# Earlier slots for the first block of a state-space recurrence inside a macaron MoE kernel

## The chip, the cores and the metric

The kernel runs on one core of a Trainium2 chip. The metric is the device time of one execution, in microseconds; several runs are given by their median. A profile is one further execution, with a record of every instruction; its span is the time from the first to the last record.

## What is computed

Input x is 4 sequences of 1024 tokens with 128 features. Three residual layers follow each other:

```python
x = x + 0.5 * ffn(layernorm(x))     # 8 experts, dense, weighted by router * gate
x = x + mamba(layernorm(x))         # selective state-space layer
x = x + 0.5 * ffn(layernorm(x))     # the same experts again
```

The FFN computes for each of 8 experts `silu(h @ w_gate) * (h @ w_up) @ w_down` (128 to 512 to 128 features) and sums the experts with per-token weights. The mamba layer projects to 256 channels, convolves along the sequence with 4 taps, applies silu, derives from the result a step width `dt` (softplus) and two 16-vectors B and C per token, and runs for each channel and each of 16 states n

```python
h = exp(dt * A[n]) * h + dt * xc * B[n];   y += h * C[n]
```

along the sequence; y is then gated and projected back.

## The kernel before, in words

The 4096 tokens are cut into 8 blocks of 512 (two per sequence, so even blocks start a sequence). An FFN pass over one block is 16 **steps**; a step handles two chunks of 128 hidden features of one expert. There are 16 passes (each block once for the first FFN, once for the second), so 256 steps, numbered from 0 here. Passes 0 to 3 are the first FFN of blocks 0 to 3; pass 4 is the second FFN of block 0, and so on.

In a step TensorE (PE) makes a gate group `pg` of six matmuls (L641 to L643, products of split fp32 numbers: high by high, low by high, high by low), an up group `pu` of six, and two `down` products `pd` of the step before (L722, plain fp32, two passes each). ScalarE (ACT) takes silu of `pg` into `h` (L625); VectorE (DVE) multiplies `h` by `pu` (L657). `pg` and `pu` have one PSUM buffer each: the gate group of the next step waits for this step's silu, the up group of the next step waits for this step's multiplication. When an expert is done ACT copies `pd` to SBUF (`take`, L735), which frees the single `pd` buffer; GpSimd (POOL) weights and sums it (L744, L747). In steps 2 to 19 and near the end the down products use split numbers as well (L697, L705), with extra work on ACT and DVE.

The mamba layer of a block is threaded between the FFN steps. Its parts in `mamba_events`: transposing (`tr`), the x projection in two halves (`xsproj`, evacuated by ACT at L909), the convolution (`conv`: first tap on ACT at L921, three taps on DVE at L931, per half), two z halves (`zproj`, L1047), `act` (silu of the convolution, L948), `xproj` (the product `dbl` at L954, evacuated by ACT at L957 and L959, its low part made by DVE at L963, and B and C sent through DRAM by SyncE, L968 and L821, to be broadcast over the partitions), `dtproj` (products `v`, ACT at L979), `softplus` (L986), `dtfin` (`dx = dt * xc`, for block 0 on DVE at L991; two ACT items for `y`, L994). Then come the states: `two` makes the exponentials of two states with four ACT instructions (L1002), here called a **bundle**. Per state DVE has a product (L1015), two scans (L1021), a copy of the last column (L1032, even blocks) and a read-out (L1033); POOL adds the result into y (L1036). All the small matmul results share one PSUM buffer, `misc`. A change of ACT function between silu, softplus and exp needs an ACT_TABLE_LOAD.

The instruction order of each engine is fixed when the program is built, by a planner. A step has four **slots** (slot = 4 x step + 0 to 3). Before each slot `run_events` runs those events of each chain that are due. An event has a slot, and may have a condition; if the condition does not hold the event waits, but at most `WAIT` = 12 slots (99 for the bundles), after which it runs regardless. `START[k]` is the base slot of block k (72 for block 0, 144 for block 1), and the tuple `FRONT[0]` (or `REST`, for other blocks) gives the offsets of ten events: `ta` transposing, `xs` x projection, `cv` convolution, `ap` act, `xp` xproj, `dp` dtproj, `sp` softplus, `df` dtfin, `n0` the first bundle. The later bundles are due at n0 + 8 * int(1.56 q). `fast` is true for block 0 only.

ACT work that is not urgent is put on a list (`plan.act_put`) and emitted when the planner sees a gap, or when somebody needs it (`act_need`); `act_run` emits it at once. DVE work goes on lists `hi` and `lo` (the states' work) and is emitted in between by planned times. Conditions that matter here: `quiet` (L1098) lets softplus run only in slots that are 5 modulo 8; `turn` (L1124) lets a bundle run only in such slots, if no softplus is wanted and no other burst has run in this slot, and if at most `QUEUE` = 9 items are on the DVE list `lo`. `exps` stores the tile of state n in `d["da", n]` (L1000), and `read` pops it again (L1028).

Of the kernel before, what the change touches and what calls it, by code (L numbers as in the profile page):

```python
# [20 lines left out]
TOL = 0.4  # L21
START = (72, 144, 232, 328, 432, 544, 656, 744)
REST = (4, 9, 17, 19, 23, 25, 29, 35, 37)
FRONT = {0: (5, 7, 8, 15, 16, 18, 21, 27, 29)}
ZT = {0: 11}
SOON = (0, 4, 6, 14, 15)
CALM = (4, 5)
# [145 lines left out]
def tile_macaron_mamba_moe(  # L173
# [32 lines left out]
    ND = DI // 128  # L206
# [11 lines left out]
    plan = Plan()  # L218

    def big(name):  # L220
        return sb.tile([P, 2, TB], F32, tag="big", bufs=BIG, name=name)
# [604 lines left out]
    riders, slot, burst_at, want = [], [0], [-1], set()  # L826
# [33 lines left out]
    def mamba_events(k):  # L860
        d = {}
# [53 lines left out]
        def conv(i):  # L915
            if i == 0:
                d["cv"] = big(f"cv_{nm}")
            cv, xs = d["cv"], d["xs"]
            assert d["xsp"] > i
            def first_tap():  # L920
                S.activation(  # L921
                    cv[:, i, :], xs[:, i, 0:TB], AF.Identity,
                    bias=cb_sb[:, i : i + 1], scale=cw_sb[:, i, 0:1],
                )
                plan.put(lambda: tap(1), 0.71, plan.act + 0.61)

            it = plan.act_put(first_tap, 0.61, 0.0)
            d.setdefault("cv_it", []).append(it)

            def tap(q):  # L930
                V.scalar_tensor_tensor(  # L931
                    cv[:, i, :], xs[:, i, q : q + TB], cw_sb[:, i, q : q + 1], cv[:, i, :],
                    ALU.mult, ALU.add,
                )
                if q < 3:
                    plan.put(lambda: tap(q + 1), 0.71)
                else:
                    d["conv"] = d.get("conv", 0) + 1
                    d["cv_at"] = plan.dve + 0.1
# [149 lines left out]
        fast = k == 0  # L1089
# [5 lines left out]
        zt = ZT.get(k, 14)  # L1095
        ta, xs, cv, ap, xp, dp, sp, df, n0 = FRONT.get(k, REST)

        def quiet():  # L1098
            if d.get("dtp") != ND or slot[0] % 8 != 5:
                return False  # L1100
            want.add(k)
            return burst_at[0] < slot[0]
# [5 lines left out]
            (xs, inproj),  # L1108
            (xs, lambda: xsproj(0), lambda: max(free(), d["xlow"][4] if d["xlow"][3] else NEVER)),
            (cv, lambda: conv(0)),  # L1110
            (xs + 2, lambda: xsproj(1), free),
            (cv + 2, lambda: conv(1)),
            (zt, lambda: zproj(0), free),
            (zt + 2, lambda: zproj(1), free),
            (ap + w, act, lambda: d["cv_at"] if d.get("conv") == ND else NEVER),
            (xp + w, xproj, lambda: max(free(), d["xc_at"])),
            (dp + w, lambda: dtproj(0), lambda: max(free(), d["low"][4] if d["low"][3] else NEVER)),
            (dp + w + 2, lambda: dtproj(1), free),
            (sp + w, softplus, lambda: 0.0 if quiet() else NEVER),
            (df + w, dtfin),  # L1120
        ]
        mid = []

        def turn():  # L1124
            fits = "dx_it" in d and slot[0] % 8 == 5 and burst_at[0] < slot[0]
            return 0.0 if fits and not want and len(plan.lo) <= QUEUE else NEVER

        for q in range(NS // 2):
            def two(q=q):
                burst_at[0] = slot[0]  # L1130
                while riders:
                    riders.pop(0)()
                exps(2 * q)
                exps(2 * q + 1)

            mid += [(n0 + 8 * int(SPR * q) + w, two, turn)]
# [103 lines left out]
```

## Time and profile before

| quantity | value |
|---|---|
| median of 3 runs | 1266.12 us (1266.01 to 1266.13) |
| time of the profiled execution | 1265.99 us |
| its span | 1264.2 us |
| POOL busy | 706.1 us, 56% |
| DMA | 115.09 MB, 91 GB/s on average |
| steps 16 to 31 (pass 1) | 85.1 us from 81.5 to 166.6 us |
| passes 2, 3, 4 | 81.4, 78.0 and 79.6 us |

The pass times are differences between the starts of the L657 multiplications of steps 16, 32, 48, 64 and 80 in the trace. Block 0's front part (transposing to softplus) lies in steps 21 to 26, its states in steps 27 to 51; block 1's front part begins at step 37.

How to read the profile: a line of the timeline has start (us from the span's start), length, engine, source line, operation, output and inputs, shape, and a count if consecutive instructions were merged; in square brackets the idle time of the engine before it and who ended it. Durations of matmuls overlap, so for PE the distance between starts is what counts. A row of the table by stages has the stage, its length, and then for PE, PE's weight loads (PEld), DVE, ACT and POOL the busy time with the number of instructions, the granted clock, and the DMA share with GB/s.

### The profile page before, as it was taken

What the parts mean: (1) busy time and instruction counts of PE and PEld (TensorE: products, weight loads), DVE (VectorE), ACT (ScalarE), POOL (GpSimd) and SP (SyncE); (2) the same over time, 40 slices, a digit from 0 to 9 for tenths busy, and PEclk for the clock granted to TensorE, in tenths of its full rate; (3) what the DMA queues carried; (4) which work ended last, traced back from release to release, by engine and by line L of the source; (5) the groups of instructions that cost most, each with busy time, mean ns of one, the idle gap of its engine ahead of it and who ended that gap; (6) DMA issues with size and microseconds to landing.
All of it is one profiled execution on the core that took longest, in us unless ns stands there. A gap on an engine that the chain in (4) does not pass through costs nothing.

```text
span 1264.2 us, 14417 instructions
## 1 busy us (share of the span) xinstructions
PE 1245.2 (99%) x4800; PEld 862.0 (68%) x4800; DVE 1138.2 (90%) x1286; ACT 921.8 (73%) x1326; POOL 706.1 (56%) x557
## 2 busy tenths in 40 slices
PE   9999999999999999999999999999999999999998
PEld 7776666666666666666666666666666666668787
DVE  6985699999899999999999999999999999998676
ACT  7684887776777768787788778778777776666653
POOL 1022465757568647775676567757775676554400
PEclk9999999999999999999999999999999999999999
DMA  4501333343343433334343353432433433311011
GB/s 147 158 26 34 107 112 86 101 112 82 81 107 97 118 91 95 93 99 110 99 100 96 92 119 84 120 98 82 113 98 79 110 92 109 103 56 42 26 43 25
DMA packets 75386, 115.09 MB, mean 91 GB/s; under 512 B 7472, under 2 KB 23728, under 8 KB 75312
## 3 DMA queue, kind: packets, MB, share of 16 engines
q1 hardware_dynamic: 75312, 114.19, 33.6%
q8 instruction: 37, 0.61, 0.2%
q14 instruction: 37, 0.30, 0.1%
HBM read 109.71 MB, written 4.46 MB: 90 GB/s over the span
## 4 chain that ended last, share of the span: by engine, by line
PE 70%; DVE 16%; ACT 5%; issue 5%; POOL 3%; DMA 1%; SPq 0%; DVEq 0%; ACTq 0%; POOLq 0%
PE pd L722 19%; PE pu L641 7%; PE pg L641 7%; PE pg L643 7%; PE pu L643 7%; PE pu L642 7%; PE pg L642 7%; DVE hb_m L1021 5%; DVE h L657 4%; PE pd L697 3%; DVE hb_m L1015 2%; DVE da_m L1033 2%; PE pd L705 1%; ACT da_m L1002 1%; ACT h L625 1%
## 5 line engine op out<-in xcount | busy, mean ns | idle before, releaser
L722 PE MATMUL pd<-h,wd 128*128 128x512 f32 x824 | 391.6, 592 | 1.2 <-ACT tmp L735 1.2
L657 DVE TENSOR_TENSOR h<-h,pu 128x1024 f32<-128x1024 f32 x256 | 311.1, 1215 | 76.9 <-PE pu L643 52.5
L1036 POOL TENSOR_TENSOR y_m<-y_m,da_m 128x1024 f32<-128x1024 f32 x128 | 310.5, 2426 | 106.5 <-DVE hb_m L1015 103.2
L625 ACT ACTIVATE h<-pg 128x1024 f32<-128x1024 f32 x256 | 262.7, 1026 | 140.2 <-PE pg L643 135.2
L641 PE MATMUL pg<-xh_f,wh 128*128 128x512 f32 x510 | 266.9, 523 | 0.7 <-ACT h L625 0.7
L744 POOL TENSOR_TENSOR tmp<-tmp,cwb 128x512 f32<-128x512 f32 x98 | 129.1, 1318 | 196.6 <-issue 106.2
L722 PEld LDWEIGHTS pd<-h,wd 128*128 128x128 f32 x824 | 153.5, 188 | 107.9 <-issue 89.6
L641 PE MATMUL pu<-xh_f,wh 128*128 128x512 f32 x512 | 205.8, 402 | 5.8 <-DVE h L657 5.6
L643 PE MATMUL pg<-xh_f,wl 128*128 128x512 f32 x510 | 201.1, 394 | 0.8 <-DVE wl L299 0.8
L643 PE MATMUL pu<-xh_f,wl 128*128 128x512 f32 x512 | 200.5, 392 | 0.0
L642 PE MATMUL pu<-xl_f,wh 128*128 128x512 f32 x512 | 199.9, 391 | 0.0
L642 PE MATMUL pg<-xl_f,wh 128*128 128x512 f32 x510 | 199.4, 391 | 0.0
L1015 DVE TENSOR_TENSOR hb_m<-dx_m,bcb_m 128x1024 f32<-128x1024 f32 x128 | 166.4, 1300 | 1.8
L1021 DVE TENSOR_TENSOR_SCAN hb_m<-da_m,st_sb,hb_m 128x512 f32<-128x512 f32 x128 | 164.2, 1283 | 2.3
L1002 ACT ACTIVATE da_m<-dt_m,A_sb 128x512 f32<-128x512 f32 x256 | 164.0, 711 | 0.6
L1021 DVE TENSOR_TENSOR_SCAN hb_m<-da_m,hb_m 128x512 f32<-128x512 f32 x128 | 156.7, 1224 | 2.6
L1033 DVE TENSOR_TENSOR da_m<-hb_m,bcb_m 128x1024 f32<-128x1024 f32 x128 | 155.8, 1217 | 1.5
L641 PEld LDWEIGHTS pg<-xh_f,wh 128*128 128x128 f32 x510 | 96.0, 188 | 64.8 <-issue 27.4
L747 POOL TENSOR_TENSOR acc<-acc,tmp 128x512 f32<-128x512 f32 x98 | 130.3, 1330 | 7.6
L642 PEld LDWEIGHTS pg<-xl_f,wh 128*128 128x128 f32 x510 | 96.3, 189 | 50.6 <-issue 36.5
L641 PEld LDWEIGHTS pu<-xh_f,wh 128*128 128x128 f32 x512 | 96.1, 188 | 35.4 <-DVE h L657 15.8
L643 PEld LDWEIGHTS pg<-xh_f,wl 128*128 128x128 f32 x510 | 95.6, 187 | 23.2 <-DVE wl L299 1.2
(181 smaller groups left out, 1494.7 us busy)
## 6 DMA issues: line engine op xcount, KB each, us to landing
bcb_m<-bc_m SPq DMA_DIRECT2D x128, 512.0 KB
cwb<-cd_f SPq DMA_DIRECT2D x128, 256.0 KB
out_dram<-x SPq DMA_DIRECT2D x13, 256.0 KB
x<-in_L_attn_x_dram SPq DMA_DIRECT2D x8, 256.0 KB
wraw<-in_L_ffn_w_gate_dram SPq DMA_DIRECT2D x8, 256.0 KB
wraw<-in_L_ffn_w_up_dram SPq DMA_DIRECT2D x8, 256.0 KB
wd<-in_L_ffn_w_down_dram SPq DMA_DIRECT2D x8, 256.0 KB
cd_f<-ct_f SPq DMA_DIRECT2D x64, 4.0 KB
```

The source lines that it names most:

```text
L625: S.activation(h, pg, AF.Silu)
L641: T.matmul(o[:, q, :], wh[e][:, i, cols[q]], d["xh"], start=True, stop=False)
L642: T.matmul(o[:, q, :], wh[e][:, i, cols[q]], d["xl"], start=False, stop=False)
L643: T.matmul(o[:, q, :], wl[e][:, i, cols[q]], d["xh"], start=False, stop=True)
L657: V.tensor_tensor(h, h, pu, ALU.mult)
L722: T.matmul(d["pd"], wd[e][:, cols], h[0], start=(f == 0), stop=(f == FC - 1))
L747: it = put(lambda: G_.tensor_tensor(acc, acc, t, ALU.add), 1.25, at)
L1002: S.activation(da[:, i, :], d["dt"][:, i, :], AF.Exp, scale=A_sb[:, i, n : n + 1])
L1015: mul = V.tensor_tensor(hb, d["dx"], bcb[:, 0:1, :].to_broadcast([P, ND, TB]), ALU.mult)
L1021: V.tensor_tensor_scan(hb[:, i, :], da[:, i, :], hb[:, i, :], 0.0 if first else st_sb[:, i, n : n + 1], ALU.mult, ALU.add,)
L1033: V.tensor_tensor(da, hb, bcb[:, 1:2, :].to_broadcast([P, ND, TB]), ALU.mult)
L1036: it = pool_put(lambda: G.tensor_tensor(d["y"], d["y"], da, ALU.add), 2.4, plan.dve)
```

## The change

Three places are edited. The offsets of block 0's front are made smaller: the front of the recurrence is due 1 to 10 slots earlier. For block 0 the first tap of the convolution is emitted on ACT at once instead of being put on the list. And two conditions for block 0 are widened: softplus may run in slots that are 1 modulo 4, and a bundle may run in such slots while `("da", 0)` is not in `d`.

```diff
-FRONT = {0: (5, 7, 8, 15, 16, 18, 21, 27, 29)}
+FRONT = {0: (4, 6, 7, 11, 12, 14, 16, 19, 19)}
...
             it = plan.act_put(first_tap, 0.61, 0.0)
+            if fast:
+                plan.act_run(it)
             d.setdefault("cv_it", []).append(it)
...
         def quiet():
-            if d.get("dtp") != ND or slot[0] % 8 != 5:
+            if d.get("dtp") != ND or slot[0] % (4 if fast else 8) != (1 if fast else 5):
                 return False
...
         def turn():
             fits = "dx_it" in d and slot[0] % 8 == 5 and burst_at[0] < slot[0]
+            if fast and ("da", 0) not in d and "dx_it" in d and slot[0] % 4 == 1:
+                fits = True
             return 0.0 if fits and not want and len(plan.lo) <= QUEUE else NEVER
```

Because the planner builds the order anew, instructions of other blocks and passes move with it. No instruction of PE, DVE, POOL or SyncE is added or removed; ACT has two ACT_TABLE_LOADs more (157 instead of 155).

## Prediction

> **What bounds the kernel now.** I read the page first, then the table by stages, then the timelines of ACT and PE around block 0's first states, and last the order in which both programs issue.
>
> ```profile
> PE 1245.2 (99%) x4800; PEld 862.0 (68%) x4800; DVE 1138.2 (90%) x1286; ACT 921.8 (73%) x1326; POOL 706.1 (56%) x557
> ```
>
> PE at 99% is not yet proof, since matmuls overlap. So I take distances between starts: a split matmul follows the one before it after 0.2275 us, an fp32 pass after 0.4285. A plain step has 12 of the first and 4 passes of the second: 12 x 0.2275 + 4 x 0.4285 = 4.44 us. Quiet steps measure 4.46 to 4.49. Summed over all matmuls (3530 x 0.2275, 864 passes x 0.4285, transposes, small products) PE needs about 1217 of the 1264.2 us. Of the rest some 5 are lost before the first step and 3 after the last; about 40 us are spread over everything, much of it as hundredths per matmul. PE is the bound everywhere; no change of order can gain more than single microseconds in a stretch of 300 us.
>
> [...]
>
> ```profile
> 81.50:166.60 85.10, 82.87 (x320) 57.19 (x319) 56.14 (x70) 59.16 (x84) 28.36 (x31) 1.00 0.24 67
> 405.60:1122.00 716.40, 710.95 (x2656) 474.60 (x2655) 683.79 (x751) 541.58 (x780) 474.88 (x358) 1.00 0.37 99
> ```
>
> The third busy time is DVE. It has 29 idle us in the 85 us in which block 0 begins, and is 95% busy later. The change uses that idle time. But the later blocks keep their own START, so a lead of block 0 is not handed on: in the issue order block 0's first product moves from step 27 to 25 and its last read-out from step 51 to 49, and from step 85 (about 420 us) on every engine issues the same instructions in the same order as before. All effect lies between 105 and 420 us.
>
> What PE waits for there is mostly ACT:
>
> ```profile
> 140.26 1.03 ACT L625 ACTIVATE h<-pg 128x1024 f32<-128x1024 f32 x1
> 141.31 1.28 ACT L518 ACT_TABLE_LOAD   x1
> 142.60 0.23 ACT L518 ACTIVATE ex_f<-ex_f 128x32 f32<-128x32 f32 x1
> 142.74 0.21 ACT L519 ACTIVATE ex_f<-ex_f 128x32 f32<-128x32 f32 x1
> 142.86 2.55 ACT L1002 ACTIVATE da_m<-dt_m,A_sb 128x512 f32<-128x512 f32 x4
> 145.42 1.28 ACT L625 ACT_TABLE_LOAD   x1
> 146.72 1.02 ACT L625 ACTIVATE h<-pg 128x1024 f32<-128x1024 f32 x1
> ```
>
> ```profile
> 145.21 1.88 PE L722 MATMUL pd<-h,wd 128*128 128x512 f32 x4
> 147.79 0.50 PE L641 MATMUL pg<-xh_f,wh 128*128 128x512 f32 x1 [0.71 <-ACT h L625]
> ```
>
> Between two silus a bundle puts 6.46 us with the router's exponentials, 6.22 without (149.50 to 155.72), against PE's 4.44. The silu then comes late. I compare each silu's start with the modelled end of its gate group: 1.77 late costs PE 0.05 us, 2.01 costs 0.30, 2.73 (146.72 above) costs 1.04. So **lateness beyond 1.73 us is a PE stall**. A late DVE does the same from about 1.6 us: 2.31 late cost 0.69.
>
> ```profile
> 249.29 0.50 PE L641 MATMUL pu<-xh_f,wh 128*128 128x512 f32 x1 [0.36 <-DVE h L657]
> ```
>
> **Stalls that exist**, as step length minus matmul content (po taken at 1.79 us): step 21 1.64, 25 0.46, 28 1.04, 33 0.60, 39 0.32, 40 0.27, 43 0.36, 45 0.22, 46 0.29, 49 0.69, 55 0.26, 63 0.72, 66 0.30, 73 0.42, 75 0.70, 78 0.30, 80 0.57: together 9.2 us.
>
> **The change part by part.**
>
> *The widened conditions.* Softplus is due at slot 72 + 16 = 88; its products are not ready until slot 98, and at slot 100 its 12 slots of patience end, so it runs there under either condition. The first bundle runs at 101, which is 5 modulo 8, so the old condition allows it too. Neither edit does what it is named for: softplus goes behind silu 24, the first bundle behind silu 25. But the read-out of state 0 pops ("da", 0), and the wide condition holds again: bundles 4 and 8 go to steps 32 and 44 (slots 129, 177), where ACT also copies `pd`. The rest (25, 27, 29, 35, 39, 41) are odd steps as before. No cost of its own: counted below.
>
> *First tap at once.* In step 21 it falls between two ACT instructions on which PE waits:
>
> ```profile
> 105.85 0.58 ACT L909 COPY xs_m<-xs_m 128x512 f32<-128x512 f32 x1 [2.36 <-PE xs_m L892]
> 106.34 0.59 ACT L735 COPY tmp<-pd 128x512 f32<-128x512 f32 x1
> 106.98 1.13 PE L722 MATMUL pd<-h,wd 128*128 128x512 f32 x2 [1.16 <-ACT tmp L735]
> ```
>
> The copy at L735 frees `pd`; in the new order the tap stands before it. Starts of a tap and of what follows it are 0.71 apart, so **+0.7** (0 to 0.81, its length).
>
> *Transposing, projections, taps, steps 21 to 25.* Same matmuls; one z half moves to step 22. Six taps in two steps make the router's `lt` in step 23 wait about 0.15 us for its low part, and the second `v` with the logits' transposes about 0.35. 0.5 against 0.46: **0**.
>
> *Softplus and bundles, steps 24 to 33.* In step 24 the second bias activation ends about 3.1 us after the gate group; from the softplus load to the next silu it takes 4.14 us (136.12 to 140.26): silu 25 is at 7.25, its gate group ends at 5.7, so 1.5 late, no stall. Then a bundle: 1.5 + 6.22 - 4.49 = 3.2 late, stall 1.5. Step 27's bundle with the router: 0.04 + 6.46 - 4.49 = 2.0, stall 0.3. Before, the same pair cost 1.04: **+0.75**. The bundle in step 32 has a `ct` and a `pd` copy before its second load (0.14 + 0.55): 6.9 against 4.55, 2.4 late, stall 0.65; the DVE stall of step 33 (0.60) goes, because DVE is ahead: **+0.05**.
>
> *Steps 39 to 50, block 1's front.* Stall at 44 to 45: 6.46 + 0.55 against 4.49, 2.55 late, 0.85. Step 46 now holds `dbl` and both `v`: the low part (L963) in step 24 ended 2.1 us after the matmul behind `dbl` began (126.48 to 128.57), and now only an up group (1.37) lies between, so 0.75, plus 0.1 for the second `v`. The projections' evacuations behind bundles at 39 and 41 cost some 0.85, the rest 0.1: 2.65. Before: 39 to 49 sum to 2.15. **+0.5**.
>
> *Steps 50 to 84.* Bundles and conv taps no longer meet in steps 62 to 66 and 73 to 75. Of 3.27 I keep 1.55 (62 0.25, 70 0.2, 73 0.2, 78 0.3, 80 0.4, small 0.2): **-1.7**.
>
> *Table loads.* Two more, each 1.28 us on ACT, which sit inside the steps counted. [...]
>
> *Queues.* On SyncE block 3's x load moves behind two state loads, but x is first read in step 31; the loads of the states are behind the same waits. POOL's work moves with its producers, and it has idle time.
>
> Sum: 0.7 + 0 + 0.75 + 0.05 + 0.5 - 1.7 = **+0.3 us**. The profiled execution took 1265.99 us, 0.13 below the median of the runs; added to the median this gives 1266.4.
>
> **Rivals.**
>
> *Faster.* DVE's idle time is the prize: at step 30 it has done some 6 us more than before (sum of its operations up to there in both orders), and whatever a late DVE costs afterwards can go. For it: 33, 43, 49, 55 and 75 are DVE stalls, 2.6 us in all. If step 33's goes without a new one at step 32 (-0.6), steps 39 to 50 cost 1.0 instead of 2.15 (-1.15) and of 3.27 behind step 50 only 0.3 stays (-2.95), then with +0.7 and +0.75 at the front: -3.25, **1262.9**. Against it: the lead shrinks while block 0 runs, block 1's taps take its place, and ACT's work per bundle is unchanged.
>
> *Slower.* The first product needs state 0's rows of B and C, which are sent after `db`. In the trace they have been issued at 129.49 and used at 143.12; the shortest distance from issue to use in all 128 is 12.27 us, with no wait shown. In the new order I get 8.9 (`db` ends about 124.1, issue 1.64 later at 125.7, first product 134.6). If the rows land later, DVE waits in order with the product in front, step 26's multiplication behind it, and PE behind that. Point of decision: DVE has 1.5 us to spare, so landing after 10.4 us. At 12.27 the wait is 3.4 us, PE loses 1.9, and the backlog of steps 26 to 29 about 1.0 more: +2.9 on the forecast, **1269.3**. From below the cost is nothing. The nearest rows: the 64 KB store before them landed within 1.62 us (its reader was issued then), and the fastest slice of the page moves 158 GB/s, at which 512 KB take 3.3 us. That is 5 us if the first load is served first, 11.5 if all three share. I take the first, at no cost.
>
> *It does nothing.* As shown, two of the edits act only by a side effect. If the moves of the others cancel to the end, 1266.1; that the stalls move from some steps to others speaks against it. It lies inside the forecast's band.
>
> **Numbers.** A measurement of this kernel can tell about 0.2% (2.5 us) from no change. Forecast, small costs against small gains: 0.62, 1266.4, its own range 1264.2 to 1268.4; nothing at all 0.08. Faster rival 0.15; slower rival 0.15. The unknown ends are the tap's 0 to 0.81, the projections' evacuations 0 to 0.85, the gain behind step 50 of 0 to 3.3, and the wait for the rows of 0 to 2.9. 8 in 10 then reach from 1263.2 to 1269.0, which takes in most of both rivals' cases. Faster by over 0.2%: 0.15, within: 0.70 (0.62 + 0.08), slower: 0.15.
>
> **What would show it.** Right: the `pd` product of step 21 starts 0.7 later behind L735; the gate group of step 27 waits 1.5 for silu 26; step 46 waits for L963; steps 43, 49 and 75 lose their DVE waits; pass 1 is longer by about 1.5 us, and steps 50 to 84 are shorter by about 1.7 in all. Wrong: DVE idle before the first L1015 with a DMA as releaser; no stall at step 27; a difference in passes after step 85, which the identical order should exclude.

## The result, and the profile after

The changed kernel takes 1269.98 us (median of 7 runs, 1268.34 to 1270.31) against 1266.01 before (7 runs, 1265.76 to 1267.41): a ratio of 1.0028 (95% interval 1.0017 to 1.0040). It is slower by 0.28%, above the forecast's own range (to 1268.4) and above its wider one (to 1269.0). The profiled execution took 1270.31 us with a span of 1268.5, 4.3 us more than before. Runs of one kernel here lie in groups some 1.4 to 1.9 us apart (of the changed kernel one at 1268.34 with a mean granted clock of 1.000, six at 1269.81 to 1270.31 with 0.998 or 0.999), for a reason that is itself a result (half-speed windows, below); so the lowest run is given beside each median.

The first line of the page of the changed kernel shows a PE that is busier by 2.2 us with as many matmuls; moved matmuls alone should not change that much (the kernel with the whole change but the tap, below, has 1246.1):

```profile
PE 1247.4 (98%) x4800; PEld 862.3 (68%) x4800; DVE 1138.6 (90%) x1286; ACT 923.8 (73%) x1328; POOL 706.0 (56%) x557
```

The table by stages says where (stage, length, busy time and count of PE, PEld, DVE, ACT, POOL, then the granted clock): pass 1, and two stretches of 4 us in step 21; then the second of these in the kernel before.

```profile
81.60:167.60 86.00, 82.68 (x313) 56.73 (x312) 59.20 (x74) 61.76 (x97) 27.34 (x31) 0.98 0.24 70
104.00:108.00 4.00, 1.95 (x10) 1.25 (x8) 2.06 (x3) 1.87 (x3) 0.02 (x1) 1.00 0.10 34
108.00:112.00 4.00, 4.00 (x8) 2.21 (x9) 0.40 (x2) 1.40 (x2) 2.80 (x3) 0.63 0.29 60
```

```profile
108.00:112.00 4.00, 4.00 (x17) 2.79 (x16) 0.19 (x1) 2.02 (x4) 1.68 (x3) 1.00 0.30 66
```

From 108 to 112 us the clock is 0.63, and PE does 8 matmuls where 17 fit before. The timeline of the changed kernel, ACT and then PE, shows what precedes it:

```profile
105.94 0.58 ACT L909 COPY xs_m<-xs_m 128x512 f32<-128x512 f32 x1 [2.36 <-PE xs_m L892]
106.62 0.81 ACT L921 ACTIVATE cv_m<-xs_m,cb_sb,cw_sb 128x512 f32<-128x512 f32 x1
107.34 0.56 ACT L735 COPY tmp<-pd 128x512 f32<-128x512 f32 x1
```

```profile
107.95 1.13 PE L722 MATMUL pd<-h,wd 128*128 128x512 f32 x2 [2.05 <-ACT tmp L735]
108.52 0.94 PE L890 MATMUL xs_m<-xh_m,win_h 128*128 128x512 f32 x1
109.25 0.63 PE L891 MATMUL xs_m<-xh_m,win_l 128*128 128x512 f32 x1
109.68 0.63 PE L892 MATMUL xs_m<-xl_m,win_h 128*128 128x512 f32 x1
```

The tap stands ahead of the copy that frees `pd`, as predicted, and PE idles 2.05 us instead of 1.16. Then the split matmuls start 0.43 us apart (109.25 to 109.68) and not 0.2275. The trace's record of the granted clock has 0.5 from 109.01 us for 3.413 us. A stretch with the clock at 0.5 is called a half-speed window here.

For everything else I keep a ledger. It takes the time of each stretch from one step's up group to the next, less its matmuls at the prediction's distances (transposes and read-outs at 0.11 us). The stretch from step 50's up group to step 51's counts as step 50. The ledger removes the effect of matmuls that moved between steps. Steps 21 to 84, profiled executions, us lost (the rows below the second are the experiments of the next sections):

| kernel | 21 | 22-29 | 30-37 | 38-49 | 50-84 | sum | median (lowest) |
|---|---|---|---|---|---|---|---|
| before | 1.61 | 1.90 | 0.91 | 2.50 | 4.74 | 11.66 | 1266.01 (1265.76) |
| changed | 4.04 | 2.29 | 1.71 | 3.15 | 4.62 | 15.80 | 1269.98 (1268.34) |
| tap only | 4.00 | 1.07 | 0.96 | 2.54 | 4.73 | 13.30 | 1267.49 (1266.07) |
| changed, 4 fillers | 1.45 | 2.26 | 1.72 | 3.12 | 4.59 | 13.13 | 1268.37 (1268.22) |
| changed, no tap | 1.61 | 5.86 | 1.73 | 3.14 | 4.56 | 16.90 | 1271.97 (1271.22) |
| changed, turn as before | 2.41 | 2.29 | 1.63 | 1.71 | 3.89 | 11.92 | 1269.11 (1268.73) |
| changed, bundle 44 to 45 | 4.06 | 2.25 | 1.71 | 1.78 | 4.32 | 14.13 | 1268.52 (1266.95) |
| changed, n0 = 27 | 2.41 | 2.28 | 0.89 | 1.75 | 6.51 | 13.84 | 1269.66 (1267.87) |
| front only | 2.41 | 1.06 | 0.96 | 2.54 | 4.66 | 11.63 | 1266.66 (1265.73) |
| before, copy first | 0.28 | 1.89 | 0.94 | 2.53 | 4.71 | 10.36 | 1266.07 (1264.44) |
| n0 = 27, copy first | 0.28 | 1.81 | 0.89 | 1.75 | 6.44 | 11.17 | 1265.44 (1265.24) |
| front only, copy first | 0.30 | 1.42 | 0.95 | 2.52 | 4.70 | 9.89 | 1264.26 (1264.05) |

The four fillers count as matmuls, some 0.9 us, so step 21 of that row lasts as long as in the rows with 2.41. Behind step 84 all rows lose the same 22.6 to 22.9 us, except two: the kernel with turn as before (25.5) and the one with bundle 45 (23.0).

The lines that answer to the prediction's chain of steps 26 to 28: in the changed kernel the first bundle stands behind the first silu after the softplus, and the silus on its two sides start 6.21 us apart.

```profile
134.21 1.02 ACT L625 ACTIVATE h<-pg 128x1024 f32<-128x1024 f32 x1
135.25 1.28 ACT L1004 ACT_TABLE_LOAD   x1
136.55 2.56 ACT L1004 ACTIVATE da_m<-dt_m,A_sb 128x512 f32<-128x512 f32 x4
139.13 1.28 ACT L625 ACT_TABLE_LOAD   x1
140.42 1.02 ACT L625 ACTIVATE h<-pg 128x1024 f32<-128x1024 f32 x1
```

The silu at 134.21 is 1.21 behind its gate group, the one at 140.42 is 2.94 behind, and PE loses 1.22. The prediction's DVE wait at 249.29 is gone; instead there is one in step 46, behind the bundle of step 44, and one in front of step 51's up group:

```profile
240.34 0.50 PE L977 MATMUL v_m<-dbs_m,wdt_h 128*128 128x512 f32 x1 [0.58 <-DVE dbs_m L965]
...
263.70 0.50 PE L641 MATMUL pu<-xh_f,wh 128*128 128x512 f32 x1 [0.80 <-DVE h L657]
```

### The profile page after: what moved, and what is told of

Same layout as the page of the kernel before. It is cut to its first block, busy times and chain, and to the rows that moved or that the text cites. A ratio compares the mean times of both kernels' runs of the same rounds, so it can differ in the third digit from the quotient of the medians.

```text
span 1268.5 us, 14412 instructions
## 1 busy us (share of the span) xinstructions
PE 1247.4 (98%) x4800; PEld 862.3 (68%) x4800; DVE 1138.6 (90%) x1286; ACT 923.8 (73%) x1328; POOL 706.0 (56%) x557
## 4 chain that ended last, share of the span: by engine, by line
PE 73%; DVE 13%; ACT 6%; issue 5%; POOL 3%; DMA 1%; SPq 0%; DVEq 0%; ACTq 0%; POOLq 0%
PE pd L722 20%; PE pu L641 7%; PE pg L641 7%; PE pg L643 7%; PE pu L643 7%; PE pu L642 7%; PE pg L642 7%; DVE hb_m L1023 4%; DVE h L657 3%; PE pd L697 3%; DVE hb_m L1017 2%; DVE da_m L1035 2%; ACT da_m L1004 2%; PE pd L705 1%; ACT h L625 1%
## 5 line engine op out<-in xcount | busy, mean ns | idle before, releaser
L1017 DVE TENSOR_TENSOR hb_m<-dx_m,bcb_m 128x1024 f32<-128x1024 f32 x128 | 168.1, 1313 | 1.8
L747 POOL TENSOR_TENSOR acc<-acc,tmp 128x512 f32<-128x512 f32 x98 | 134.4, 1372 | 7.6
```

Of the source, the lines that this page charges most:

```text
L747: it = put(lambda: G_.tensor_tensor(acc, acc, t, ALU.add), 1.25, at)
L1017: mul = V.tensor_tensor(hb, d["dx"], bcb[:, 0:1, :].to_broadcast([P, ND, TB]), ALU.mult)
```

## The experiments: the tap and the clock

Theory A: the change loses by two things that the prediction lacked, a half-speed clock window behind step 21's longer wait, and bundles of the side effect that collide with block 1's front. Rival B: the earlier offsets themselves crowd block 0's work, and the collisions only move. Rival C: time gained or lost in step 21 is eaten by slack behind it.

**Filling the wait** (`e1_fill`): the changed kernel, and

```diff
+            if fast and i == 0:
+                fill = ps.tile([P, 2, TB], F32, tag="pg", bufs=1, name="fill")
+                for q in range(9):
+                    T.matmul(fill[:, 0, 0:P], ident, ident, start=True, stop=True)
```

> The changed kernel with nine small matmuls (128x128, into the free gate buffer, never read) that PE does in step 21 while it waits for the copy that frees pd. Nothing else moves. Theory A (the changed kernel's step 21 costs more than the tap's own delay because PE, idle for over 2 us, is granted a lower clock for about 4 us afterwards, which costs 1.7 us): the clock stays at 1.00, the matmuls behind the wait are 0.23 us apart again, the wait itself stays; about 1268.3 us, 2.3 above the kernel before. Rival B (the slow matmuls at 108.5 to 112.5 us have another cause, the memory or the order): no change, 1270.0 us.

Median 1269.63 (lowest 1268.38). In the profile the window is gone (clock 1.00 from 104 to 116 us) and PE is 1.82 us ahead of the changed kernel up to its last matmul; but the span ends 5.2 us behind the issue of the last two stores and not 3.6. The page counts one more load of instructions, of 16 KB, and the trace has it at 1264.5 us, between that issue and the end:

```profile
q8 instruction: 38, 0.62, 0.2%
```

The nine fillers cost at the end what they saved, so the test said nothing by its median. Four of them (`e8_fill4`) were to leave the 38th load out:

> The changed kernel with four small fp32 matmuls of the identity (not nine) into a free product buffer in step 21; their result is not used. They take about 0.9 us of the 2.05 us that TensorE waits there, so that it idles about 1.1 us as before. The nine of the first experiment made a 38th instruction load of 16 KB fall at the very end (1264.5 us), and the last store landed 1.65 us later; four should leave it out. Theory A (idle time in a window halves the clock): no half-speed window in most runs, 1268.3, which is 1.6 below the changed kernel. Rival B (order alone sets the time): 1269.9, or later by the filler's length.

Median 1268.37, nine of ten runs below 1268.5: A, to the tenth. The copy comes as late as in the change, but the fillers take 1.05 us of the wait, so PE idles 1.16 us as in the kernel before, and the clock is 1.00 from 104 to 116 us:

```profile
105.58 1.05 PE L912 MATMUL fill<-ident 128*128 128x128 f32 x8
107.80 1.13 PE L722 MATMUL pd<-h,wd 128*128 128x512 f32 x2 [1.16 <-ACT tmp L735]
108.36 0.79 PE L890 MATMUL xs_m<-xh_m,win_h 128*128 128x512 f32 x1
108.99 0.39 PE L891 MATMUL xs_m<-xh_m,win_l 128*128 128x512 f32 x1
```

**Lengthening the wait** of the kernel before, by copying `pd` in step 21 twice or three times:

```diff
-            S.copy(t, pd)
+            for _ in range(2 if (s, e) == (1, 1) else 1):
+                S.copy(t, pd)
```

> The kernel before with the pd copy (L735) of step 21 made twice, so that PE is idle there for about 1.6 us instead of 1.2. Theory A with its point below 1.6: +0.5 for the wait and +1.7 for the clock, 1268.2 us. Theory A with its point above 1.6, and rival B: +0.5, 1266.5 us, clock 1.00.

> The kernel before with the pd copy of step 21 made three times: PE idle for about 2.1 us, as long as in the changed kernel, with nothing else of the change in it. Theory A: +1.0 for the wait and +1.7 for a lowered clock, 1268.7 us, with matmuls at twice their distance for some 4 us behind the wait. Rival B: +1.0, 1267.0 us.

Medians 1267.35 (lowest 1266.45) and 1268.48 (1267.03). The profiled runs lose 0.6 and 1.3 us in step 21, which stays to the end (against C), and have no window there (clock 1.00 from 104 to 116 us), although PE waits 1.78 us in the one and 2.40 in the other, longer than in the change:

```profile
109.62 1.13 PE L722 MATMUL pd<-h,wd 128*128 128x512 f32 x2 [2.40 <-ACT tmp L736]
```

So the length of the wait alone does not decide, and in these two profiles A as it was put failed; what else decides is not shown. The second profile has a half-speed window in the first steps (clock 0.61 from 8 to 12 us, 0.96 from 12 to 16). The times fall into groups: five runs of the first kernel at 1266.5 to 1266.8 (clock 0.999 or 1.000) and five at 1267.9 to 1268.3 (0.998). Which of the slower ones had their window in step 21 only a profile could tell.

**The tap alone** (`e4_tap_only`), before with `if fast: plan.act_run(it)` behind `act_put`:

> The kernel before with only the first taps emitted at once (old offsets, old conditions). Theory A: the wait in step 21 and the lowered clock come with this edit alone, +2.4 us, and the rest of the order moves little: about 1268.4 us, with +-1 for the moved steps. Rival C (the loss sits in the crowded bundles of the earlier offsets): no more than the tap's own 0.7 to 1.0, 1267.0 us.

Nine runs at 1267.4 to 1267.6 and one at 1266.07; the profiled one has the window (clock 0.96 from 104 to 108 us, 0.61 from 108 to 112). Without it the tap costs nothing in the end: its 0.8 us in step 21 come back in steps 22 to 29 (1.07 for 1.90), because the planner now puts the softplus into step 25, alone between two silus, and the pair of steps 26 and 28 loses 0.3 instead of 1.0.

**The change without the tap** (`e6_no_tap`):

> The changed kernel with the first taps placed as before; the earlier offsets and both widened conditions stay. Theory A: TensorE's wait in step 21 is again near 1.2 us, no half-speed window follows, so the time is that of the one changed run without a window, 1268.3, less what of the tap's 0.97 us isn't regained later: 1267.4 to 1268.3. Rival B (the window is an accident of that run and not tied to the wait): windows still fall in most runs, 1269 or more.

Median 1271.97: wrong for A, and right for B by the number alone, since no window falls in its profile (mean clock 1.000). But with the earlier `xproj` the convolution is late: `dbl` waits 2.67 us in step 23 and the stretch loses 3.8. In the change the tap at once is what makes the earlier offsets bearable.

**Copy first** (`e7_before_take`): the kernel before, with the copy that frees `pd` ahead of the first projection's evacuation:

```diff
             plan.need(lambda: d["xlow"][3])
+            if fast and i == 0:
+                for o in list(ffn.values()):
+                    if "take" in o:
+                        plan.act_need(o["take"])
```

> The kernel before with one edit: in step 21 the copy that frees pd goes on ScalarE ahead of the first transposed projection's evacuation, so that TensorE's wait for pd (1.16 us) goes. Theory A (the wait is real time on TensorE, and nothing else is due there): step 22 starts about 1.2 us earlier and the end moves by as much: 1264.9. Rival C (steps 25 to 29 have bundles that come late anyway, and slack in front of them is eaten there, as the tap's delay was regained at step 29 in the tap-only kernel): 1265.7 to 1266.0.

Step 21 loses 0.28 for 1.61, and every later stretch is as before: the ledger refutes C for this edit. Yet the median is 1266.07: three runs at 1264.4 to 1264.7, seven at 1266.0 to 1266.3. The profiled one is of these, with a half-speed window at the start (clock 0.59):

```profile
8.00:12.00 4.00, 3.61 (x9) 2.88 (x10) 1.72 (x4) 1.80 (x3) 0.00 (x0) 0.59 1.01 330
```

## The experiments: the bundles and the front

**The widened turn taken out** (`e5_no_wide`; the two lines that set `fits = True` for block 0 are left out):

> The changed kernel without the widened condition on bundles: first taps at once and the earlier offsets stay, bundles go back to odd steps only. Theory A (two causes: the half-speed clock window behind step 21's longer wait, and the bundles that the widened condition puts into steps 32 and 44): the window stays (matmuls 0.43 us apart at about 109 us), steps 32 to 34 and 44 to 46 and the late VectorE at step 50 lose their stalls, about 2 us; median near 1267.7. Rival B (the earlier offsets themselves cost it: softplus, router and bundles meet more closely, whichever steps the bundles take): the stalls of steps 31 to 51 appear in other steps and the median stays at 1269.5 to 1270.

By the median it looks like B. The ledger says otherwise up to step 84: 11.92, of which 0.8 are the tap's, so the bundles of the widened turn cost 1.4 us in steps 38 to 49 and 0.7 in 50 to 84. But here the order does not meet that of the other kernels again until step 157, and behind step 84 it loses 2.8 us more. So the median can't decide between A and B: the time of a kernel whose order differs to step 157 can't price an edit in step 44.

**Only the bundle of step 44 moved** (`e9_w32`), order equal from step 85:

```diff
-            if fast and ("da", 0) not in d and "dx_it" in d and slot[0] % 4 == 1:
+            if fast and ("da", 0) not in d and "dx_it" in d and slot[0] % 4 == 1 and slot[0] < 150:
```

> The changed kernel with the widened condition ended at slot 150: the bundle of step 32 stays, the one of step 44 goes to step 45, block 1's v products to step 47 and its softplus to step 49; from step 85 on the same order as both kernels. Theory A (the bundle in step 44 pushes block 1's projections into one step, where TensorE waits 1.9 us for their low part, and softplus and bundles then follow so closely that VectorE is late at step 50, 1.0 us): both go, and the median falls by about 2.5 us to 1267.5, or 1265.9 in runs without a half-speed window. Rival B (the losses of steps 46 to 51 come from the earlier offsets and only move): 1269.5 to 1270.

Lowest run 1266.95, median 1268.52, with the window in 7 of 10 by the times: 1.4 us below the changed kernel in both. Steps 38 to 49 fall from 3.15 to 1.78 and the loss in front of step 51 (1.02) goes; 0.7 comes new in step 54, and 0.3 behind step 84. A has the place right; the size that it expected was 2.5.

**Only the bundles' offset back** (`e10_n27`), `FRONT` ending in 27 for 19:

> The changed kernel with only the last of the earlier offsets, that of the bundles, put back near its old value (27 for 19): taps, projections and softplus are as early as in the change, the first two bundles are in steps 25 and 27 as well, the third in step 31 and no bundle in an even step. Theory A: steps 25 to 29 keep their loss (1.2 + 0.3), steps 30 to 51 lose no more than before; 1267.9 with the half-speed window, 1266.2 without. Rival B: 1269.5 to 1270.

Lowest 1267.87: 1.7 above A's 1266.2. Steps 30 to 49 do lose less than before (2.64 for 3.41), but steps 50 to 84 lose 6.51 for 4.74, most of it in steps 56, 66 and 70. Here B is right: the loss moved.

**Only the front** (`e11_front`), `FRONT` (4, 6, 7, 11, 12, 14, 18, 21, 29), taps at once, turn as before (the softplus condition stays widened):

> Only the early part of block 0: first taps at once and the earlier offsets up to the projections; softplus falls into step 25 (18, 21), the bundles have their old offset and steps (27, 29, 31 ...), without the widened condition. Issue order from step 29 on as before. Theory A: the softplus now has a step of its own between silus, so of the 1.68 us lost in steps 24 to 28 before only the 0.3 of the bundle with the router stays: 1.3 us less, against 0.8 us more in step 21 and 1.7 of a half-speed window in most runs: 1267.1, and 1265.4 in runs without. Rival B: the window or the collisions are not tied to these places; 1268 or more.

Lowest 1265.73, median 1266.66. Steps 22 to 29 gain 0.84 (expected 1.3: the projections' waits in step 24, 0.45, were left out), step 21 loses 0.80: nothing is left. But for the window in step 21 its rows are those of the tap alone.

**With the copy first**: `e12_n27_take` (offset 27) and `e13_front_take` (front only, and `quiet` as before so that the softplus stays in step 25). The second against the kernel before, without the lines of the copy shown above:

```diff
-FRONT = {0: (5, 7, 8, 15, 16, 18, 21, 27, 29)}
+FRONT = {0: (4, 6, 7, 11, 12, 14, 18, 21, 29)}
...
             it = plan.act_put(first_tap, 0.61, 0.0)
+            if fast:
+                plan.act_run(it)
```

> As the kernel with the offset 27, and with the copy that frees pd ahead of the first transposed projection's evacuation in step 21. Theory A: the wait of step 21 goes (2.05 us), and with it the half-speed window: 1.3 us less than the runs without a window of the offset-27 kernel, 1264.9. Rival C (the steps behind eat it): 1266.

> The early part of block 0 alone (first taps at once, earlier offsets up to the projections), the copy that frees pd ahead of the evacuation in step 21, softplus in step 25 and the bundles in their old steps 27, 29, 31 ...; issue order from step 29 on as before. Theory A: the wait of step 21 goes (1.3 us), the projections lose 0.5 in step 24 as in the run with offset 27 and the copy ahead, and of the 1.68 us of steps 24 to 28 some 0.7 stay: 1.3 - 0.5 + 1.0 = 1.8 us less than before in runs without a half-speed window: 1264.1 median. Rival C (what the front gains is eaten behind it): 1265.3 or more. From step 30 on no difference between the two orders.

The first has a median of 1265.44, ratio 0.9994 (0.9985 to 1.0004): steps 21 to 49 lose 2.2 us less than before, and steps 50 to 84 take 1.7 of it. The second has 1264.26 against 1266.13, ratio 0.9986 (0.9977 to 0.9995), and beats both kernels. In its timeline `pd` follows the first projection with no wait:

```profile
105.24 0.40 PE L892 MATMUL xs_m<-xl_m,win_h 128*128 128x512 f32 x1
105.47 1.02 PE L722 MATMUL pd<-h,wd 128*128 128x512 f32 x2
106.31 0.50 PE L890 MATMUL xs_m<-xh_m,win_h 128*128 128x512 f32 x1
```

**The start** (`e14_front_take_idle`): the same, `range(14)` for `range(12)` warm-up matmuls, to see whether fewer runs are slow when PE waits less ahead of the first transposes (0.55 us in its profile, 1.23 in that of `e13_front_take`).

> The same with 14 warm-up matmuls at the start for 12. [...]

Median 1264.34, ratio 0.9983 (0.9974 to 0.9992), all eleven runs from 1264.10 to 1264.51; with 12 two of eleven were at 1266.0 and 1266.3. Two in eleven against none is too few to show that the two matmuls changed anything.

## Why the prediction was wrong

The ledger's difference of 15.80 - 11.66 = 4.1 us is the span's 4.3 but for 0.2 outside these steps. Against the prediction's terms:

- **First tap, +0.7**: the order cost 0.80 (2.41 for 1.61 in three kernels without a window there). The order's price was right, but the step failed for a term that it did not have: the wait of 2.05 us brought a half-speed window, 4.04 - 2.41 = 1.63 us more. `e8_fill4` shows it, with a wait of 1.16 us and a clock of 1.00. This is the largest of the three misses.
- **Steps 21 to 25, 0, and softplus with bundles, +0.75**: +0.39 in steps 22 to 29. The stalls are those foreseen (1.22 for 1.5, 0.29 for 0.3); a 0.36 of before in step 25 went as well.
- **Steps 32 and 33, +0.05**: +0.80 in steps 30 to 37. This step failed too. The DVE stall went as stated (0.49 to 0.04), the bundle of step 32 cost 0.86 for 0.65 (the lines below), and the bundle of step 35, right behind the normalization of the next blocks, made silu 36 2.10 late, 0.38 that was not in the sum; the rest is small.

```profile
171.65 1.28 ACT L625 ACT_TABLE_LOAD   x1
172.94 1.02 ACT L625 ACTIVATE h<-pg 128x1024 f32<-128x1024 f32 x1
174.02 0.50 PE L641 MATMUL pg<-xh_f,wh 128*128 128x512 f32 x1 [0.28 <-ACT h L625]
```

- **Steps 39 to 50, +0.5**: +0.65. Right, with its two main places: 0.78 at steps 44 to 45 for 0.85, and 1.1 in step 46 for 0.85, of which the wait for the low part is 0.86 with the slow start of the matmul behind it.
- **Steps 50 to 84, -1.7**: -0.12. This is the third step that failed: half of the stalls there were taken to go, and nearly as much came new. Losses did go at 54 to 55, 63, 66, 74 and 80, but 62 and 73 kept 0.65 and 0.68 where 0.25 and 0.2 were left to them, and in front of step 51 a new 1.02 appeared: silu 50 1.79 late behind the bundle of step 49, DVE's multiplication 2.66 late. `e9_w32` shows that this one belongs to the bundle of step 44. In the same microseconds DVE's product (L1017) took 2.13 us instead of 1.22 and POOL's L747 2.16 instead of 1.27; whether one stretches the other was not tested.

```profile
256.54 2.13 DVE L1017 TENSOR_TENSOR hb_m<-dx_m,bcb_m 128x1024 f32<-128x1024 f32 x1
260.19 1.02 ACT L625 ACTIVATE h<-pg 128x1024 f32<-128x1024 f32 x1
```


The three failed terms are 1.7, 0.75 and 1.6 us: together 4.05, more than the miss of 3.8 (4.1 for 0.3); the other terms came out 0.2 smaller in all. The slower rival gave nearly the right time, 1269.3, but by a mechanism that did not occur, so its number is luck: the rows of state 0 were issued at 127.52 us and first used at 136.41, the 8.9 us that were foreseen, and DVE shows no wait there. The identical order after step 85 was right, 22.7 us lost in both. So was the reading that the widened turn acts by a side effect: the bundles in steps 32 and 44 did cost. That the widened softplus condition changes nothing was read from the order; no run took it alone out of the change.

What stays open: why two orders that differ by one bundle in step 44 lose 4.62 and 4.32 us in steps 50 to 84, and a third 6.5. Each is a sum of ten small collisions, which I could list behind the run but not foresee.

## What to carry to other kernels

When one engine bounds a kernel, follow its idle time in front of each moved instruction: the useful edit here was to free a single buffer first (1.3 us by the ledger), not to start a chain earlier. A relief that is put down as a gain must be laid out collision by collision in the new order, or counted as zero: here new collisions took the place of nearly all of it. Compare orders that meet again soon after the edit, and count losses by stretch, before a median is believed as the price of one line.

## What the runs showed of the hardware

**Half-speed windows.** In the profile of the changed kernel the granted clock is 0.5 for 3.413 us, from 109.01 us on, behind a wait of PE of 2.05 us. In it split matmuls start 0.43 us apart (109.25 to 109.68), elsewhere 0.2275. The same wait of 2.05 us stands ahead of the window in the profiles of the tap alone (clock 0.61 from 108 to 112 us) and of bundle 45 (split matmuls 0.42 us apart, 109.25 to 109.67). A wait of 1.16 us had none behind it: 1.00 from 104 to 116 us in the kernel before and in the one with four fillers. But neither had the waits of 1.78 and 2.40 us of the copies made twice and three times, also with 1.00 from 104 to 116 us. Windows also stand in the first steps of some profiles: from 8 to 12 us the clock is 0.61 with the tripled copy and 0.59 with the copy first, and 1.00 in the kernel before, the changed one, and those of `e1_fill`, `e2_gap1` and `e4_tap_only`. Three more kernels with the tap at once lose 2.41 us in step 21 in their profiles, for 4.00 to 4.06 in the three with the window (ledger above). And the same program may or may not pay for one: of seven runs of the changed kernel six took 1269.81 to 1270.31 us at a mean clock of 0.998 or 0.999, and one 1268.34 at 1.000. So here the tap at once came with a window in step 21 in three profiles of six, and the fillers took the window away from the changed kernel's; what decides beyond the length of the wait is not shown.

**A 38th load of instructions at the end.** With nine fillers (18 more matmuls and 18 more weight loads) the profile counts 38 loads of instructions for 37, and the one more, of 16 KB, is among the transfers behind the issue of the last two stores. From that issue the packets go on for some 3.4 us (1263.08 to between 1266.4 and 1266.6) and the span for 5.2; in the changed kernel it is 2.2 (1264.89 to 1267.06) and 3.6. With four fillers the median was 1268.37 for 1269.63. That the load delays the stores is read from their order in one profile, not tested apart.
